# Two 1x1 convolutions of neighbouring blocks: seven products for eight in the earlier one too, and their matmuls taken in turn

## The chip, the cores and the metric

The kernel runs on one core of one Trainium2 chip. The metric is the device time of one execution in microseconds (us). All runs quoted here are with a mean granted TensorE clock of 0.98 unless another is given. Engine names in the profile: PE is TensorE's matmuls, PEld its weight loads, DVE is VectorE, ACT is ScalarE, POOL is GpSimd, SP is SyncE. L123 is a line of the kernel. A record is one matmul instruction of the trace; an fp32 matmul leaves two. PSUM is the memory that TensorE writes its sums to, in banks.

## The reference

Two bottleneck blocks on 64 images of 14x14 with 1024 channels, all in fp32, with batch statistics over images and pixels:

```python
def block(x, w1, b1, g1, be1, w2, b2, g2, be2, w3, b3, g3, be3, residual_scale):
    out = relu(_bn(_conv(x, w1, b1, 1, 0), g1, be1))     # 1x1, 1024 -> 256
    out = relu(_bn(_conv(out, w2, b2, 1, 1), g2, be2))   # 3x3, 256 -> 256
    out = _bn(_conv(out, w3, b3, 1, 0), g3, be3)         # 1x1, 256 -> 1024
    out = softplus(residual_scale)[0] * out
    return relu(x + out)
# ... the second block takes the first one's result
```

## The kernel before

The pixels are cut into 32 tiles of two images, 392 pixels each. A tile of `x` is 128 partitions x 8 channel groups x 392. The stages follow one another on TensorE: first convolution of block 0; 3x3 convolution; a transposing stage that forms the Gram matrix, from which the last convolution's statistics are computed before it is run; then the **fused stage**, in which the last convolution of block 0 is finished, added to `x`, and taken at once as input by the first convolution of block 1; then the 3x3 convolution, the transposing stage and the last convolution of block 1.

The last convolution in the fused stage is plain: eight output rows a tile, each from two matmuls, evicted by VectorE and ScalarE.

```python
def residual(psum, pool, b, t, w3, aff, made=()):
    scale, shift = aff
    xt = load_x(pool, b, t)
    yield xt
    for o in range(CS):                       # CS = 8
        ps = made[o] if o < len(made) else conv3(psum, t, o, w3)
        v = xt[:, o, :]
        nc.vector.scalar_tensor_tensor(v, ps, scale[:, o : o + 1], v, ALU.mult, ALU.add)
        nc.scalar.activation(v, v, AF.Relu, bias=shift[:, o : o + 1])
        # ... after the last row: write the tile
        yield xt
```

The first convolution already uses Winograd's form of Strassen's scheme: it treats a pair of tiles as the two columns of a 2x2 block product, and makes seven products, p1 to p7, instead of eight; each is four matmuls. Products p1, p6, p7 and p4 pile up on one PSUM bank, with a copy of the sum so far (a save) taken by ScalarE between them; p5 and p3 pile up on another.

```python
before, xn = None, next(rest)
for t in range(0, T, 2):                      # pairs of tiles
    # ... last convolution of tile t, p4 and p3 of the pair before
    now = Conv1(psum, pool, (xa, xb), (t, t + 1), w1, par[b + 1], stats1)
    # ... last convolution of tile t + 1
    now.p1(); now.p2(); now.p5(); now.t23(); now.p6()
    # ... first row of tile t + 2
    now.p7(); now.c22()
    before = now
```

## Time and profile before

| | before |
|---|---|
| time, median of 3 runs | 2219.84 us |
| first convolution, block 0, starts to 3x3 convolution's start | 7.1 to 320.8 us |
| 3x3 convolution to the start of the transposing stage | 320.8 to 667.1 us |
| transposing stage, statistics | 667.1 to 773.3 us |
| fused stage, first to last matmul | 773.3 to 1406.1, 632.8 us |
| what follows | 1406 to 2217 us |

The stage limits are the starts of the first matmuls of each stage in the trace. How the stage is bound, the prediction shows. In addition, three rows of the page's table of the costliest groups (line, engine, operation, out<-in, shapes, count, then busy time, mean ns of one, then idle time before them and what ended it). They hold both blocks' last convolutions: 512 output rows of 392 pixels in all, with 4 records each.

```profile
L126 PE MATMUL ps<-y,w 128*128 128x392 f32 x2048 | 685.6, 494 | 0.2 <-DVE x L515 0.2
...
L515 DVE SCALAR_TENSOR_TENSOR x<-ps,scale,x 128x392 f32<-128x392 f32 x512 | 316.0, 624 | 274.8 <-PE ps L126 273.5
L516 ACT ACTIVATE x<-x,shift 128x392 f32<-128x392 f32 x512 | 314.7, 622 | 435.5 <-DVE x L515 435.5
```

### The profile page before, as it was taken

Reading aid. Unit: us, or ns where it says so; the run is one execution under the profiler, and the core shown is the slowest. Engines: PE = TensorE matmul, PEld = TensorE weight load, DVE = VectorE, ACT = ScalarE, POOL = GpSimd, SP = SyncE. Lnnn points to the kernel's source line nnn. Section 1 sums busy time; section 2 is a strip of 40 time slices with the busy share of each in tenths; the row PEclk is TensorE's granted clock in tenths of the full one; section 3 lists DMA queues with packets and bytes.
Section 4 is the critical chain, followed back from the end, with each engine's and each line's share of the span. In section 5 each row is a group of like instructions: output and inputs, shape, how many; then the busy total and the mean of one; then the engine's idle time right before and its main releaser. Section 6 shows DMA issues by size and latency. Waiting matters only on the chain.

```text
span 2217.4 us, 22513 instructions
## 1 busy us (share of the span) xinstructions
PE 2144.0 (97%) x8984; PEld 1578.6 (71%) x8984; DVE 1343.1 (61%) x2091; ACT 585.8 (26%) x943; POOL 60.9 (3%) x126
## 2 busy tenths in 40 slices
PE   8999979999989999999999999799999799999997
PEld 5555559999988855555555555599999797555554
DVE  4766567787775455554555555678878534444443
ACT  1111142111105032332223323511111221444443
POOL 0100000000001000000000000000000000000000
PEclk9999989999999999999999999899999899999999
DMA  7755425555543443443434432355555401778884
GB/s 276 267 204 206 176 84 190 187 193 190 187 158 121 159 167 149 171 175 145 175 152 171 171 146 116 148 186 194 190 186 194 195 12 59 291 290 302 306 319 176
DMA packets 43977, 409.13 MB, mean 185 GB/s; under 512 B 5216, under 2 KB 5472, under 8 KB 11104
## 3 DMA queue, kind: packets, MB, share of 16 engines
q1 hardware_dynamic: 29376, 286.80, 35.9%
q0 software_dynamic: 13056, 118.50, 13.1%
q10 hardware_dynamic: 1440, 2.40, 0.3%
q8 instruction: 71, 1.16, 0.2%
q14 instruction: 34, 0.28, 0.0%
HBM read 289.18 MB, written 118.49 MB: 184 GB/s over the span
## 4 chain that ended last, share of the span: by engine, by line
PE 83%; issue 12%; DVE 2%; ACT 1%; POOL 1%; DMA 1%; POOLq 0%; ACTq 0%; DVEq 0%; SPq 0%
PE ps L126 19%; PE bu L126 15%; PE bp L126 7%; PE ps L343 6%; PE ps L349 6%; PE ps L338 6%; PE ps L345 6%; PE ps L351 6%; PE bx L126 4%; PE bx L439 4%; PE bp L440 2%; PE ps L451 2%; ACT y L264 1%; POOL out L519 1%; DVE spare L155 0%
## 5 line engine op out<-in xcount | busy, mean ns | idle before, releaser
L126 PE MATMUL ps<-y,w 128*128 128x392 f32 x2048 | 685.6, 494 | 0.2 <-DVE x L515 0.2
L126 PEld LDWEIGHTS ps<-y,w 128*128 128x128 f32 x2048 | 390.4, 191 | 285.9 <-issue 2.8
L515 DVE SCALAR_TENSOR_TENSOR x<-ps,scale,x 128x392 f32<-128x392 f32 x512 | 316.0, 624 | 274.8 <-PE ps L126 273.5
L516 ACT ACTIVATE x<-x,shift 128x392 f32<-128x392 f32 x512 | 314.7, 622 | 435.5 <-DVE x L515 435.5
L371 DVE TENSOR_TENSOR f<-ps,ms 128x448 f32<-128x448 f32 x192 | 113.2, 600 | 148.3 <-PE ps L351 81.8
L338 PE MATMUL ps<-sums,u 128*128 128x224 f32 (+1 forms) x768 | 172.1, 347 | 25.4 <-DVE sums L318 12.7
L126 PE MATMUL bu<-t,w1s 128*128 128x392 f32 x496 | 173.6, 493 | 1.3 <-ACT u L189 1.3
L343 PE MATMUL ps<-r,u 128*128 128x224 f32 (+1 forms) x768 | 173.6, 347 | 0.0
L349 PE MATMUL ps<-r,u 128*128 128x224 f32 (+1 forms) x768 | 172.8, 346 | 0.0
L338 PEld LDWEIGHTS ps<-sums,u 128*128 128x128 f32 x768 | 137.3, 190 | 26.8 <-issue 13.3
L345 PE MATMUL ps<-r,u 128*128 128x192 f32 (+1 forms) x768 | 154.1, 322 | 0.0
L351 PE MATMUL ps<-r,u 128*128 128x192 f32 (+1 forms) x768 | 153.3, 321 | 0.0
L362 ACT ACTIVATE ms<-ps 128x448 f32<-128x448 f32 (+1 forms) x80 | 41.9, 524 | 391.7 <-PE ps L338 391.7
L126 PEld LDWEIGHTS bu<-t,w1s 128*128 128x128 f32 x496 | 94.1, 190 | 71.0 <-ACT u L189 2.8
L343 PEld LDWEIGHTS ps<-r,u 128*128 128x128 f32 x768 | 141.8, 190 | 1.3
L349 PEld LDWEIGHTS ps<-r,u 128*128 128x128 f32 x768 | 136.7, 189 | 1.4
L345 PEld LDWEIGHTS ps<-r,u 128*128 128x128 f32 x768 | 132.9, 189 | 1.2
L351 PEld LDWEIGHTS ps<-r,u 128*128 128x128 f32 x768 | 131.8, 188 | 1.0
L189 ACT ACTIVATE u<-bu 128x392 f32<-128x392 f32 x93 | 46.2, 497 | 303.2 <-PE bu L126 303.2
L439 PE MATMUL bx<-zt 128*128 128x257 f32 x392 | 119.3, 386 | 4.1 <-DVE zt L453 4.0
L453 DVE TENSOR_TENSOR zt<-ps,crow 128x512 f32<-128x512 f32 x98 | 66.2, 690 | 93.3 <-PE ps L451 93.2
L264 ACT ACTIVATE y<-y,shift,scale 128x1568 f32<-128x1568 f32 x64 | 103.6, 1682 | 6.4 <-DVE shift L556 6.4
(134 smaller groups left out, 2115.3 us busy)
## 6 DMA issues: line engine op xcount, KB each, us to landing
u<-u SPq DMA_DIRECT2D x96, 1280.0 KB, 5.5
x<-in_x SPq DMA_DIRECT2D x62, 1568.0 KB, 6.7
mid<-x POOLq DMA_DIRECT2D x32, 1568.0 KB, 5.5
x<-mid SPq DMA_DIRECT2D x32, 1568.0 KB, 8.5
out<-x POOLq DMA_DIRECT2D x32, 1568.0 KB, 7.7
u<-y POOLq DMA_DIRECT2D x24, 320.0 KB, 5.9
u<-spare POOLq DMA_DIRECT2D x24, 320.0 KB, 3.0
x<-in_x SPq DMA_DIRECT2D x4, 784.0 KB, 7.2
```

The source lines that it names most:

```text
L126: tc.keep_in_program_order(nc.tensor.matmul(*args, **kw))
L264: nc.scalar.activation(y, y, AF.Relu, bias=shift[:, s : s + 1], scale=scale[:, s : s + 1])
L338: nc.tensor.matmul(m[:, o, :n], w(s, D1D2), sums[:, s].rearrange("p l c -> p (l c)"), start=(s == 0), stop=(s == MS - 1),)
L343: nc.tensor.matmul(odd, w(s, D1), r[:, s, :, WH:], start=(s == 0), stop=False)
L345: nc.tensor.matmul(odd[:, :, : WH - 1], w(s, D3), r[:, s, :, WH + 1 :], start=False, stop=(s == MS - 1))
L349: nc.tensor.matmul(even, w(s, D2), r[:, s, :, :WH], start=(s == 0), stop=False)
L351: nc.tensor.matmul(even[:, :, 1:], w(s, D0), r[:, s, :, : WH - 1], start=False, stop=(s == MS - 1))
L371: nc.vector.tensor_tensor(f[:, o].rearrange("p r (i q c) -> p q (r i) c", i=GI, q=2)[:, :, :lines], eos[o][:, :, :n].rearrange("p q (l c) ...
L439: nc.tensor.matmul(g0, zt[:, c, 0:P], zt[:, c, :], start=first, stop=last)
L453: nc.vector.tensor_tensor(zt[:, :, :M], tp.rearrange("p (c m) -> p c m", c=CH), crow[:, None, :].to_broadcast([P, CH, M]), ALU.subtract,)
L515: nc.vector.scalar_tensor_tensor(v, ps, scale[:, o : o + 1], v, ALU.mult, ALU.add)
L516: nc.scalar.activation(v, v, AF.Relu, bias=shift[:, o : o + 1])
```

## The change

The last convolution of the fused stage gets the seven-product scheme too, with the two halves of a tile (196 pixels) as columns and four groups of two output rows. The first convolution is done inside one tile as well. A product of the last convolution is a single matmul, so the products that pile up on one bank follow closely on each other. To give the saves time, the matmuls of the two convolutions are taken in turn, one of each, with the last convolution `LAG` = 12 steps ahead (after its first tile). In the changed kernel's profile, tiles whose names begin with `c` belong to the last convolution, those with `a` to the first; `cy` and `ay` are the banks of p1, p6, p7 and p4, `cx` and `ax` those of p2, `cp` and `ap` those of p5 and p3.

```diff
+LAG = 12
...
+    def stream(items):
+        before = None
+        for now in items:
+            yield from now.p1()
+            if before is not None:
+                yield from before.p3()
+                yield from before.p4()
+            yield from now.p6()
+            yield from now.p2()
+            yield from now.p5()
+            yield from now.p7()
+            before = now
...
+    class Conv3(Seven):
...
+        def after1(self):
+            self.saved(self.u12[:, : self.n], 0)        # ScalarE, 196
+        def after6(self):
+            self.saved(self.u12[:, self.n :], 0)        # ScalarE, 196
+        def after2(self):
+            self.add(0, 0, self.x)                      # VectorE, 196
+        def after5(self):
+            self.add(1, 1, self.p)
+        def after7(self):
+            u3 = self.saved(..., 1)
+            nc.gpsimd.tensor_add(self.part(1, 1), self.part(1, 1), u3)
+        def after3(self):
+            self.add(0, 1, self.p)
+            v = self.xt[:, self.o[0], :]
+            nc.gpsimd.tensor_add(v, v, self.u12)        # 392
+            self.relu(0)                                # ScalarE, 392
+        def after4(self):
+            self.add(1, 0, self.y)
+            self.relu(1)
...
+        a, c = stream(first_convs()), stream(last_convs())
+        step = 7 * CS // 2
+        for i in range(step + LAG):
+            next(c)
+        while True:
+            more = next(a, "end"), next(c, "end")
```

Besides: the first stage uses `stream` too, which changes the order of its products (before, p4 stood ahead of p3 there, and the next pair's p1 between p6 and p7); the fused stage's tiles are written by DMAs that ScalarE issues, before by GpSimd's; the row `crow` used in the transposing stage is no longer loaded with the parameters at the start but by its own DMA at that stage; the weights' sums for the seven products are made near the end of the transposing stage.

## The prediction

> **What bounds the kernel now.** I read the page's shares first, then the table of stretches of the fused stage (last convolution of block 0 with first convolution of block 1), then its timeline. TensorE is busy 97% of the span:
>
> ```profile
> PE 2144.0 (97%) x8984; PEld 1578.6 (71%) x8984; DVE 1343.1 (61%) x2091; ACT 585.8 (26%) x943; POOL 60.9 (3%) x126
> ```
>
> The stretches (TensorE, weight loads, VectorE, ScalarE, GpSimd busy us, clock, DMA) show the whole stage and one period of it, two tiles:
>
> ```profile
> 774.00:1407.00 633.00, 631.16 (x1912) 363.21 (x1910) 338.26 (x450) 189.31 (x321) 17.01 (x32) 1.00 0.40 155
> 845.21:884.71 39.50, 39.50 (x121) 22.80 (x121) 20.88 (x28) 11.85 (x20) 1.06 (x2) 1.00 0.44 163
> ```
>
> TensorE has no gap, at full clock; VectorE works 53% and ScalarE 30% of a period. A period is 32 matmuls of the last convolution and 28 of the first, 392 columns each; an fp32 matmul is two records, so 120 records in 39.50 us, 0.329 us a record. Sixteen periods are 632 us. Only fewer columns through TensorE can shorten this stage, and only while nothing stops TensorE.
>
> The timeline (start, duration, engine, line, instruction) gives the prices of what the change will use:
>
> ```profile
> 400.30 0.83 PE L351 MATMUL ps<-r,u 128*128 128x192 f32 x4
> 400.97 0.73 PE L338 MATMUL ps<-sums,u 128*128 128x168 f32 x4
> 401.54 0.74 PE L343 MATMUL ps<-r,u 128*128 128x168 f32 x4
> ...
> 779.69 3.29 DVE L515 SCALAR_TENSOR_TENSOR x<-ps,scale,x 128x392 f32<-128x392 f32 x6
> 780.34 3.29 ACT L516 ACTIVATE x<-x,shift 128x392 f32<-128x392 f32 x6 [1.72 <-DVE x L515]
> ...
> 1397.54 2.90 PE L126 MATMUL bu<-t,w1s 128*128 128x392 f32 x8 [0.65 <-ACT u L189]
> ```
>
> Starts of successive groups: 192 columns take 0.67/4 = 0.168 us a record, 168 take 0.57/4 = 0.143. So 196 columns are not limited by weight loads and take about 0.168. Six ReLUs back to back take 3.29 us and one 0.622 (page), so each further one 0.534. The last row is a product that accumulates on a bank and had to wait until ScalarE had saved the partial sum there: this dependence exists already, but with products of eight records it comes up only at the stage's end.
>
> The GpSimd hand-over, from VectorE's last write to GpSimd's start:
>
> ```profile
> 1755.43 0.86 DVE L402 TENSOR_TENSOR y<-fb,f 128x672 f32<-128x672 f32 x1
> ...
> 1756.48 0.19 POOL L433 MEMSET zt<- 128x2 f32 x4 [367.98 <-DVE y L402]
> ```
>
> 0.19 us. In the same timeline TensorE's handing over a bank to VectorE or ScalarE took 0.20 to 0.26 us after the next product's start, ScalarE to TensorE 0.05 (1397.49 to 1397.54) plus 0.10 for the exposed weight load (2.90 against 2.80 us), VectorE to ScalarE 0.03.
>
> **What the Trainium skill says.** "ScalarE: Activation LUTs", What ACT_TABLE_LOAD costs: 186 ns plus 0.833 ns an element, 93 ns more for each per-partition operand, and 93 ns of overlap back to back. For a ReLU of 392 that is 606 ns; the trace has 622, and an overlap of 88. For the new saves of 196 columns with a per-partition scale it gives about 0.44 us. "GPSIMD Engine Reference", 3.1: a two-input add takes about 2.6 cycles an element at 1.2 GHz. No GpSimd add is in this trace. My estimate from it: 392 elements 0.85 us plus the 0.10 that a tiny memset costs in the trace, 0.95 us; 196 elements 0.52. "TensorE: Matmul & The Clock Gate", table at the top: ScalarE, VectorE and GpSimd take their queues in strict order. The trace before neither contradicts nor tests it. "SBUF — State Buffer", Who interferes with whom: a VectorE instruction with two SBUF inputs contends with a GpSimd one that reads SBUF. Not shown here yet.
>
> **The change, part by part.**
>
> *Columns.* A tile's last convolution becomes 4 groups of 7 products, each one matmul of 196 columns: 28. The first convolution is now done inside one tile, 28 matmuls of 196. So 56 x 2 x 0.168 = 18.8 us a tile against 19.75; times 32, 602 against 632: 30 us less. That is 1.4%, and with nothing else it's all there is. The first stage keeps 28 matmuls of 392 a pair in another order; its gaps allow it, so zero. Combining the weights moves into the transposing stage, where VectorE was half idle; it frees some 2 us at the fused stage's start, but the first new save waits for the scale where eight plain matmuls ran on. Zero together.
>
> *Evictions.* For each group: 3 saves by ScalarE, 4 multiply-adds of 196 by VectorE (0.624 less 196/0.96 ns = 0.42 us each), 2 adds by GpSimd, 2 ReLUs. Per tile ScalarE gets 4 x (3 x 0.35 + 2 x 0.534) = 8.5 us plus 1.5 for the first convolution; VectorE 6 plus some 7; GpSimd 4 x 1.5 = 6. None is full in 18.8 us. Throughput isn't the trouble, order is.
>
> *The order.* The built program takes the two convolutions' matmuls strictly in turn, so a step of the last convolution is 0.67 us. Steps of a group n, with b the group before: p1(n), p3(b), p4(b), p6(n), p2(n), p5(n), p7(n). Products p1, p6, p7, p4 pile up on one bank, and each may start only after ScalarE saved the sum so far. ScalarE's queue of the built program reads, for nearly every group:
>
> ```
> save of p1(n); relu row 1 of b (waits GpSimd); relu row 2 of b; save of p6(n); save of p7(n)
> ```
>
> So the save that p7(n) needs stands behind two ReLUs, and the first of these waits for a GpSimd add that waits for VectorE. With 0 at the end of p3(b): VectorE starts at 0.23, done 0.65; GpSimd starts 0.84, done 1.79; first ReLU at 1.84; two ReLUs, 1.07: the save starts at 2.91, ends 3.35; TensorE goes on with p7(n) at 3.50. In a full pipeline p7(n) would start nine matmuls after 0, 9 x 0.336 = 3.02. A stall of 0.48 us in each group, and since the next p3 follows p7(n), it doesn't shrink: the period is 14 x 0.336 = 4.70 plus 0.48.
>
> To that: in two of four groups the queue holds a save or result of the first convolution before the p6 save too, 0.26 us, so 0.13 on average; at a tile's start VectorE's queue has the first convolution's 784-element sums (half of 1.79 us) between the adds, which I put at 0.3 us a tile, 0.08 a group; contention of those sums with GpSimd, 0.07 by guess. Sum 0.76 us a group.
>
> *Count.* 128 groups, of which about 6 run alone before the first convolution joins, and 122 in turn: 122 x 0.76 = 93 us. The six alone are nominally 7 x 0.336 = 2.35 us each, but the same chain (save of p7 behind the ReLUs, then p4) takes 3.5: 6 x 1.2, with the start 9 us. Net: -30 + 93 + 9 = +72, so 2220 + 72 = 2292 us.
>
> **The rivals.** (1) *The gain comes through.* The stall is a difference of two near numbers, 3.50 and 3.02. If the GpSimd add takes 0.5 us instead of 0.95, the save is ready in time, and the time is 2190 to 2205. For it: the add's duration is not in the profile, and whoever ordered the queues thought the ReLUs ready early. Against: in the groups of instructions GpSimd's one single-input operation on 128 elements a partition took 0.287 us, and a memset of 2 elements 0.10, which makes 1.5 ns an element and 0.69 us for 392 without the second input. That case leaves about 0.2 us, and 2255 us. (2) *VectorE's queue is the brake*: the add to a bank that p3 accumulates on stands behind sums that wait for the last ReLU of the tile. I count 0.3 us of it a tile; were it 1.5, 2330. (3) *GpSimd is the bound*: only if its adds average over 2.3 us (8 in 18.8); then the stage is over 700 us as well. (4) *DMA*: 0.44 of its share in a period; tile loads and writes stay, the writes issued by ScalarE. Not a bound.
>
> **Range and chances.** The GpSimd add decides: 0.1 us of it is 12 us of the kernel. 0.7 to 1.2 us gives 2260 to 2325. Below, I leave room for rival 1, above for rivals 2 and 3: 2215 to 2335. Faster by over 2% needs 44 us where 30 are on offer: 0.02. Within 2% (up to 2264): 0.31. Slower: 0.67.
>
> **What would show it.** Right: records of 196 columns 0.168 us apart where nothing waits; a wait of TensorE's `cy` bank on ScalarE's `cu` of near 0.5 to 0.8 us in nearly every group, some 90 us in all; ScalarE's ReLU waiting for GpSimd; TensorE near 85% busy in the stage; stage 700 us. Wrong: a GpSimd add of 0.5 us or less and TensorE still at 99%; or TensorE's waits put down to VectorE instead; or a changed time in another stage.

## The result, and the profile after

The changed kernel takes 2284.53 us (median of 4 runs, 2282.97 to 2284.69), against 2220.11 us (2219.68 to 2220.56) for the kernel before in the same rounds. Its ratio is 1.0289, with a 95% interval of 1.0271 to 1.0306: slower. A ratio here is the mean time of one kernel's fast runs over the mean of the other's in the same rounds, so it isn't quite the ratio of the medians.

The two traces, compared by the start of each stage's first matmul:

| | before | after | longer by |
|---|---|---|---|
| first convolution, block 0 | 313.7 | 318.2 | 4.5 |
| 3x3 convolution to transposing stage | 346.3 | 350.8 | 4.5 |
| transposing stage, statistics | 106.3 | 108.8 | 2.5 |
| fused stage, first to last matmul | 632.8 | 686.9 | 54.1 |
| the rest, to the end | 811.3 | 811.4 | 0.1 |

The first matmul came 0.4 us earlier, so the sum of 65.7 is 65.4 at the end (spans 2217.4 and 2282.8 us).

TensorE's shares, from the page of the changed kernel:

```profile
PE 2159.3 (95%) x10648; PEld 1804.8 (79%) x10648; DVE 1445.2 (63%) x2591; ACT 725.8 (32%) x1391; POOL 249.6 (11%) x350
```

The stretches of the fused stage (TensorE, weight loads, VectorE, ScalarE, GpSimd busy, clock, DMA), the whole and 50 us of it:

```profile
785.00:1471.00 686.00, 643.01 (x3581) 588.97 (x3580) 434.18 (x940) 328.37 (x768) 205.58 (x256) 0.99 0.37 144
1000.00:1050.00 50.00, 47.33 (x268) 43.58 (x267) 31.76 (x69) 24.58 (x59) 15.04 (x19) 1.00 0.42 162
```

Instead of 633 us without a gap there are 686 with 643 busy. Even this flatters TensorE. A product's busy time reaches 0.16 us beyond the next product's possible start (a pair of records takes 0.49 us and the next may start after 0.33), so a gap of that size isn't seen in it. Count records instead: 268 in 50 us, 0.187 us a record, where 0.166 us is the distance of undisturbed ones. That makes 11% of lost time, not the 5% that the busy share suggests.

What TensorE and the others waited for in the fused stage, from the table of waits (engine, tile, line, what released it: total us, times, longest):

```profile
ACT x L336 <- POOL x L357: 234.4, 127, 2.4
...
PEld cy L135 <- ACT cu L323: 59.3, 132, 3.5
...
PEld ap L135 <- issue: 21.3, 32, 1.3
PE cy L135 <- ACT cu L323: 17.9, 34, 2.9
...
PEld cp L135 <- DVE x L331: 14.3, 32, 0.5
PE ap L135 <- DVE y L273: 12.6, 32, 1.0
```

PEld and PE wait for the same thing at the same time, so their rows aren't to be added. I therefore took the matmul starts of the trace: each distance over 178 ns, less the 166 ns of an undisturbed record, put down to the tile of the later record.

| what TensorE was about to do in the fused stage | us lost | of it in the stage's beginning |
|---|---|---|
| last convolution's p6 and p7 (tile `cy`, combined weights): wait for ScalarE's saves | 53.4 | 7 |
| first convolution's p3 (tile `ap`): waits for VectorE's result of the same bank | 20.2 | |
| last convolution's p3 (tile `cp`): waits for VectorE's add of the same bank | 13.5 | |
| all else | 5.4 | |
| sum | 92.5 | |

The other 594.4 us are its 3584 records at 0.1658 us; together 686.9, which is the stage. Not all of the sum is waiting: up to 793 us the granted clock was 0.50, and 12 distances of 0.33 us there make about 2 us of it.

One group's chain, from the timeline (start, duration, engine, line, instruction). The prediction drew this chain from the built program and the prices of before:

```profile
1007.16 0.49 PE L135 MATMUL cp<-y,w3s 128*128 128x196 f32 x2
...
1007.70 0.42 DVE L331 SCALAR_TENSOR_TENSOR x<-cp,scale,x 128x196 f32<-128x196 f32 x1 [1.41 <-PE cp L135]
...
1008.20 1.01 POOL L357 TENSOR_TENSOR x<-x,cu 128x392 f32<-128x392 f32 x1 [0.73 <-DVE x L331]
...
1009.25 1.13 ACT L336 ACTIVATE x<-x,shift 128x392 f32<-128x392 f32 x2 [1.73 <-POOL x L357]
...
1010.29 0.40 ACT L323 ACTIVATE cu<-cy,scale 128x196 f32<-128x196 f32 x1
...
1010.74 0.30 PEld L135 LDWEIGHTS cy<-ct,w3s 128*128 128x128 f32 x2 [0.40 <-ACT cu L323]
1010.74 0.60 PE L135 MATMUL cy<-ct,w3s 128*128 128x196 f32 x2
```

Product p3 of the group before starts at 1007.16; VectorE adds it; GpSimd adds the saved row; ScalarE does two ReLUs; only then comes the save of the running sum (1010.29), and p7 starts at 1010.74. Ten matmuls after p3 it could have started at 1007.16 + 10 x 0.332 = 1010.48. The p6 product whose sum is saved here was at 1008.49, so the bank had been ready from about 1009.0. The save waited for the queue, not for its data.

Where the group stood in its tile made a difference: by the four groups of a tile, p7 lost 0.37, 0.37, 0.68 and 0.13 us on average between 830 and 1400 us. The 0.68 is the group with a result of the first convolution (0.31 us more in ScalarE's queue) in front of the save, as at 1003.92 to 1005.27 in the same timeline; the 0.13 is the group in which the first convolution's p3 had just been waited for.

The two groups of instructions that the chain is made of, from the page, with their means:

```profile
L336 ACT ACTIVATE x<-x,shift 128x392 f32<-128x392 f32 x256 | 148.1, 614 | 234.4 <-POOL x L357 234.4
...
L357 POOL TENSOR_TENSOR x<-x,cu 128x392 f32<-128x392 f32 x128 | 129.8, 1014 | 204.3 <-DVE x L331 204.2
```

Outside the fused stage, the 4.5 us ahead of the transposing stage go with one wait, again in the timeline:

```profile
663.38 0.46 ACTq L794 DMA_DIRECT2D crow<-in_par  x1
...
672.89 0.29 DVE L795 TENSOR_SCALAR crow<-crow 128x256 f32<-128x256 f32 x1 [4.83 <-DMA crow<-in_par]
```

Here VectorE's maximum on `crow` stands in its queue in front of the small instructions that make the scale for the whole stage, and `crow` takes 9 us from issue to use.

### The profile page after: what moved, and what is told of

It reads as the page before. It is cut to its first block, busy times and chain, and to the rows that moved or that the text cites. A ratio compares the mean times of both kernels' runs of the same rounds, so it can differ in the third digit from the quotient of the medians.

```text
span 2282.8 us, 27264 instructions
## 1 busy us (share of the span) xinstructions
PE 2159.3 (95%) x10648; PEld 1804.8 (79%) x10648; DVE 1445.2 (63%) x2591; ACT 725.8 (32%) x1391; POOL 249.6 (11%) x350
## 4 chain that ended last, share of the span: by engine, by line
PE 54%; issue 21%; DVE 9%; ACT 7%; POOL 6%; DMA 2%; ACTq 0%; POOLq 0%; DVEq 0%; SPq 0%
PE ay L135 8%; PE ps L465 6%; PE ps L460 6%; PE ps L471 6%; PE ap L135 5%; PE ps L467 5%; PE ps L473 5%; ACT x L336 5%; POOL x L357 4%; PE cy L135 4%; DVE x L331 3%; PE ax L135 2%; ACT cu L323 2%; PE bx L561 2%; PE cp L135 1%
## 5 line engine op out<-in xcount | busy, mean ns | idle before, releaser
L135 PE MATMUL ps<-y,w 128*128 128x392 f32 x1024 | 340.3, 495 | 0.0
L135 PEld LDWEIGHTS ps<-y,w 128*128 128x128 f32 x1024 | 195.8, 191 | 143.4 <-issue 2.7
L635 DVE SCALAR_TENSOR_TENSOR x<-ps,scale,x 128x392 f32<-128x392 f32 x256 | 160.3, 627 | 174.8 <-PE ps L135 154.7
L336 ACT ACTIVATE x<-x,shift 128x392 f32<-128x392 f32 x256 | 148.1, 614 | 234.4 <-POOL x L357 234.4
L135 PE MATMUL ay<-at,w1s 128*128 128x196 f32 (+1 forms) x752 | 209.3, 381 | 2.2 <-ACT au L259 2.2
L323 ACT ACTIVATE cu<-cy,scale 128x196 f32<-128x196 f32 x384 | 160.1, 418 | 109.0 <-PE cy L135 104.9
L331 DVE SCALAR_TENSOR_TENSOR x<-cp,scale,x 128x196 f32<-128x196 f32 x256 | 107.1, 418 | 109.2 <-PE cp L135 109.2
L135 PEld LDWEIGHTS ay<-at,w1s 128*128 128x128 f32 x752 | 136.3, 190 | 36.3 <-ACT au L259 3.2
L135 PE MATMUL cy<-ct,w3s 128*128 128x196 f32 x512 | 140.8, 357 | 23.2 <-ACT cu L323 17.1
L357 POOL TENSOR_TENSOR x<-x,cu 128x392 f32<-128x392 f32 x128 | 129.8, 1014 | 204.3 <-DVE x L331 204.2
L465 PEld LDWEIGHTS ps<-r,u 128*128 128x128 f32 x768 | 141.8, 190 | 1.3
L471 PEld LDWEIGHTS ps<-r,u 128*128 128x128 f32 x768 | 136.2, 188 | 1.4
L467 PEld LDWEIGHTS ps<-r,u 128*128 128x128 f32 x768 | 132.8, 189 | 1.2
```

What stands on the lines that cost most here:

```text
L135: tc.keep_in_program_order(nc.tensor.matmul(*args, **kw))
L323: nc.scalar.activation(v, self.y, AF.Identity, scale=self.scale[:, o : o + 1])
L331: nc.vector.scalar_tensor_tensor(v, bank, self.scale[:, o : o + 1], v, ALU.mult, ALU.add)
L336: nc.scalar.activation(v, v, AF.Relu, bias=self.shift[:, o : o + 1])
L357: nc.gpsimd.tensor_add(v, v, self.u12)
L465: nc.tensor.matmul(odd, w(s, D1), r[:, s, :, WH:], start=(s == 0), stop=False)
```

## The experiments

Twelve kernels, in three rounds. The changed kernel is the base unless another is named. All had 3 rounds beside the kernel before, whose medians there were 2221.40, 2220.67 and 2220.33 us. "Lost" is always by matmul starts, as in the table above.

### e1: ReLUs behind the save

```diff
         def after3(self):
             self.add(0, 1, self.p)
             nc.gpsimd.tensor_add(v, v, self.u12)
-            self.relu(0)
         def after4(self):
             self.add(1, 0, self.y)
-            self.relu(1)
-            self.end()
+        def late(self):            # called after p7 of the next group,
+            self.relu(0)           # and held in program order
+            self.relu(1)
+            self.end()
```

> The two ReLUs of a group are put behind the next group's p7 save in ScalarE's queue; nothing else is touched. Theory (order of ScalarE's queue): TensorE's wait for the save before p7, 46 us over the fused stage by the gaps between matmul starts, falls under 10 us, and the time by 35 to 50 us, to 2235 to 2250. Rival (VectorE's queue is the brake, the ScalarE waits only hide it): the waits move to the banks that VectorE reads and the time changes by less than 10 us. Rival (narrow matmuls are slow in themselves): no change.

Measured: 2245.37 us, ratio 1.0105 (1.0090 to 1.0120), and a **wrong result** (relative error 0.29), so this one is a look at the timing only. The fused stage took 648.3 us. From its table of waits:

```profile
PEld cp L135 <- DVE x L337: 41.4, 31, 1.4
...
PEld cy L135 <- ACT cu L329: 9.0, 14, 3.4
```

The loss at `cy` fell from 53.4 to 9.1 us and that at `ap` from 20.2 to 1.9; that at `cp` rose from 13.5 to 40.6. So the order in ScalarE's queue was the brake on p7; e7 repeats this with a correct result. The error comes from the first tile's first convolution having no p3 and p4 of a predecessor: its stream is eight matmuls shorter there, every later tile begins that much earlier, and by a count of the program's steps this is two steps before the last ReLUs of its tile are issued.

### e2: the row add on VectorE

```diff
-            nc.gpsimd.tensor_add(v, v, self.u12)
+            nc.vector.tensor_add(v, v, self.u12)
```

> The 392-element add of the saved sums goes from GpSimd to VectorE; ScalarE's queue keeps its order. Theory: the first ReLU becomes ready some 0.55 us earlier (about 0.55 us on VectorE for 0.08 hand-over and 1.01 on GpSimd), more than the stall of 0.35 to 0.4 us before p7, so that wait falls from 46 to under 10 us; VectorE gets 2.2 us more a tile, which may add up to 15 us to its own waits: 2235 to 2260. Rival (VectorE's queue is the brake): more work in it makes the kernel slower, 2290 to 2330.

Measured: 2256.73 us, ratio 1.0159 (1.0142 to 1.0176), correct; fused stage 659.5 us. The loss at `cy` fell to 10.3 us, at `ap` it doubled to 40.0, at `cp` it stayed at 12.2. Taking the GpSimd add out of the chain is worth about as much to p7 as moving the ReLUs, and the work comes back in VectorE's queue. The expectation's "keeps its order" isn't quite so: in the trace a result of the first convolution has changed places with a ReLU in ScalarE's queue once a tile, so this test is not of one link alone.

### e5: the first convolution's sums held in VectorE's order

```diff
-            nc.vector.tensor_sub(self.t3, self.b[1][1], self.b[0][1])
+            tc.keep_in_program_order(nc.vector.tensor_sub(self.t3, ...))
             # the same for t2 and t1
```

> The first convolution's sums t1 to t3 stand behind the previous item's result in VectorE's queue instead of before it. Theory: TensorE's wait for the bank ap before the first convolution's p3 goes, 18 to 20 us in the fused stage and 4 us in the first stage, the p7 waits stay near 46 us: 2258 to 2268. Rival: the wait only moves to the last convolution's banks, because the sums still wait for a ReLU with VectorE's queue behind them: within 8 us of 2284.

Measured: 2295.79 us, ratio 1.0335 (1.0319 to 1.0351), correct. Theory and rival both failed. The first stage lost 17 us more (the 3x3 convolution starts at 341.9 us instead of 324.9), and the fused stage gained only 3.8 (683.1): 17.0 us at `ap`, 23.5 at `cp`, 44.3 at `cy`. The trace doesn't bear out the rival's reason either: VectorE stands idle before none of the pinned sums (looked at from 6 to 342 and from 800 to 1400 us). In the first stage the results that the sums now stand behind wait for ScalarE's saves (69.0 us in 15 waits, in the changed kernel 4.6 in one), and TensorE waited for the late sums (13.3 us in 5 waits at `ay`). In the fused stage `ap` still waits with the sums behind it; e13 looks at that again. The edit also moved two pairs of ScalarE's instructions a tile, among them a save and a ReLU, so the smaller loss at `cy` is not the sums' alone.

### e6: the maximum of `crow` on GpSimd

```diff
-                    nc.vector.tensor_scalar(crow, crow, 0.0, None, ALU.max)
+                    nc.gpsimd.tensor_scalar(crow, crow, 0.0, None, ALU.max)
```

> The maximum of the separately loaded row is taken on GpSimd, so that VectorE's queue no longer waits for that load in front of the affine of the second normalization. Theory: the start of the first transposing stage moves back by 4.5 us, of the second by 0.6 us: 2278 to 2281. Rival: another load ends at the same time and nothing changes.

Measured: 2279.30 us, ratio 1.0259 (1.0244 to 1.0275), correct: 5.2 us less than the changed kernel, where the intervals of the ratios just overlap (1.0271 and 1.0275). From its timeline:

```profile
673.17 0.86 POOL L795 TENSOR_SCALAR crow<-crow 128x256 f32<-128x256 f32 x1 [11.34 <-DMA crow<-in_par]
```

The DMA is no quicker, but now an idle engine waits for it. The transposing stage starts at 671.0 instead of 675.7 us and the fused stage, at 687.2 us long as before, at 780.4 instead of 784.5. Of the 4.7 us 0.6 were given back: TensorE ran at a granted clock of 0.50 for the first 10 us of the stage (671 to 681), where in the changed kernel that took 5 us.

### e4: a lead of 19 instead of 12

```diff
-LAG = 12
+LAG = 19
```

> The changed kernel with one number altered: the last convolution runs 19 matmuls ahead of the first one's stream instead of 12, that is one group of seven more (the two streams keep their places against each other within a group). Theory: of the idle time of TensorE in the fused stage, only what comes from the tile boundary goes: the last convolution's p3 waiting for VectorE's add behind the sums (13.5 us) and some of the first convolution's p3 waiting for its result (20 us); the wait of p7 for ScalarE's saves behind the ReLUs (53 us with the start) stays between 42 and 56 us, so the fused stage takes 660 to 678 us and the kernel 2258 to 2276. Rival: the lead itself is what starves TensorE; then the p7 wait falls as well and the kernel takes under 2245. Second rival: the places within a period don't matter; 2280 to 2290. A fill that is 7 matmuls longer alone costs about 1 us in all of them. Results correct.

Measured: 2301.64 us, ratio 1.0366 (1.0349 to 1.0384), correct; fused stage 705.2 us. All three expectations failed. `ap` did fall to 2.8 us, but `cp` rose to 19.1 and `cy` from 53.4 to 82.5. By groups of a tile, p7 lost 0.37, 0.68 and 0.37 us as in the changed kernel, and in the group at the tile's boundary 1.09 instead of 0.13. That group in the timeline:

```profile
1020.53 0.49 PE L135 MATMUL cp<-y,w3s 128*128 128x196 f32 x2
1020.80 0.98 DVE L246 TENSOR_TENSOR at<-x 128x784 f32<-128x784 f32 x1 [1.67 <-PE ap L135]
...
1021.70 0.42 DVE L331 SCALAR_TENSOR_TENSOR x<-cp,scale,x 128x196 f32<-128x196 f32 x1
...
1022.25 1.01 POOL L357 TENSOR_TENSOR x<-x,cu 128x392 f32<-128x392 f32 x1 [4.67 <-DVE x L331]
```

VectorE waits 1.67 us to write the next tile's sum, because TensorE still reads the last tile's from the one buffer (tile `ap`); the add that p3 started (1020.53) stands behind that sum until 1021.70, and everything in the chain behind it is late by as much. The lead doesn't only decide how early a tile is ready; it decides what stands next to what in three queues.

### e7: e1 and e4 together

Late ReLUs and `LAG = 19`; no other edit. The ReLUs of a tile are then issued before the first convolution reads it.

> The late ReLUs of e1 and the lead of 19 together. In e1 the first convolution of a tile read the tile before its last ReLUs; with a lead of 19 they are issued before it, so the result must be correct now (relative error as that of the kernel before). Theory: the p7 wait stays under 12 us as in e1, the wait of the last convolution's p3 for VectorE (40.6 us in e1, because the sums in VectorE's queue waited for the late ReLUs) falls under 12, the wait of the first convolution's p3 under 8; the fused stage takes 608 to 626 us and the kernel 2205 to 2223. Rival: VectorE's queue still waits for the late ReLUs at each tile's start, since the sums are issued as soon as the tile's first convolution begins; then the p3 wait stays over 25 us and the kernel takes 2235 to 2255.

Measured: **2210.61 us**, ratio 0.9954 (0.9939 to 0.9969), correct. Fused stage 613.2 us, 19.6 less than before the change: 9.5 us lost at `cy`, 4.5 at `ap`, 1.5 at `cp`. The same stretch of 50 us as above, and then the group of the ReLUs:

```profile
1000.00:1050.00 50.00, 50.00 (x303) 49.66 (x302) 36.88 (x79) 26.39 (x64) 18.22 (x22) 1.00 0.44 166
```

```profile
L342 ACT ACTIVATE x<-x,shift 128x392 f32<-128x392 f32 x256 | 143.6, 610 | 0.7 <-POOL x L363 0.7
```

There are 303 records where the changed kernel had 268, and no gap. ScalarE's wait for GpSimd in front of the ReLUs went from 234.4 to 0.7 us. VectorE still waits for TensorE's reading of the sum as in e4 (40.1 us in 31 waits, 1.3 each), but no save stands behind what waits for it, and TensorE no longer feels it. Each half of this edit alone is a failure: 17 us slower, or a wrong result.

### e9: the row add on VectorE, with the lead of 19

The edits of e2 and e4 together.

> The lead of 19, and the row add of 392 on VectorE instead of GpSimd (as in e2). Theory: p7 wait 8 to 15 us as in e2; of e2's wait of the first convolution's p3 (40.0 us) and of the last one's (12.2) half goes with the lead: fused stage 625 to 645 us, kernel 2222 to 2242. Rival: the 40 us are due to the work that the adds put into VectorE's queue (4 x 0.5 us a tile) wherever the tile's boundary stands: 2248 to 2260. Results correct.

Measured: 2244.97 us, ratio 1.0109 (1.0093 to 1.0124), correct; fused stage 647.2 us, both just beyond the theory's upper ends, and under the rival's. `ap` fell from 40.0 (in e2) to 2.8 us, while `cy` rose from 10.3 to 28.2 and `cp` from 12.2 to 19.3. So the 40 us at `ap` hung on where the tile's boundary stood, but more than half of it came back elsewhere.

### e8: the ReLUs on GpSimd, with the lead of 19

```diff
-            nc.scalar.activation(v, v, AF.Relu, bias=self.shift[:, o : o + 1])
+            nc.gpsimd.tensor_scalar(v, v, self.shift[:, o : o + 1], 0.0, ALU.add, ALU.max)
```

> The lead of 19, and the ReLU moved from ScalarE to GpSimd (one tensor_scalar: plus shift, maximum with 0), which so does both row adds and ReLUs. Theory: ScalarE's queue then holds only saves and results that wait for TensorE alone, so the p7 wait falls under 12 us. GpSimd gets per group 1.01 + 0.60 + two ReLUs of 392 elements, which I put at 0.6 to 0.8 us each: 2.8 to 3.2 us of a group's 4.7, so it is not the bound. Fused stage 608 to 630 us, kernel 2205 to 2228. Rival: GpSimd's two ReLUs stand before the next group's add and before the bank of GpSimd's own order, and contention with VectorE slows its sums, so the waits for VectorE (first convolution's p3) grow over 30 us: 2240 to 2265. Results correct.

Measured: 2376.21 us, ratio 1.0700 (1.0684 to 1.0716), correct; fused stage 781.8 us, clock 0.958. Both expectations failed on one number:

```profile
L336 POOL TENSOR_SCALAR x<-x,shift 128x392 f32<-128x392 f32 x256 | 463.0, 1817 | 15.0
```

I had put this instruction at 0.6 to 0.8 us; it takes 1.82. A group then needs 1.01 + 0.60 + 2 x 1.82 = 5.25 us of GpSimd, against 14 matmuls x 0.332 = 4.65, so GpSimd alone makes the stage longer than before: 672 us for 128 groups. It was busy 43 of 50 us in the same stretch, and the stage took 781.8; what keeps it idle for the rest (it waits for VectorE and ScalarE before the add of 196) no run isolates. I had priced a two-step instruction like a one-step one.

### e10: the row add in two halves

The changed kernel with its lead of 12 and its ReLUs where they were; only the half row that is ready after p2 is added then, so that the add in p7's chain has 196 elements instead of 392.

```diff
         def after2(self):
             self.add(0, 0, self.x)
+            v = self.part(0, 0)
+            nc.gpsimd.tensor_add(v, v, self.u12[:, : self.n])
         def after3(self):
             self.add(0, 1, self.p)
-            v = self.xt[:, self.o[0], :]
-            nc.gpsimd.tensor_add(v, v, self.u12)
+            v = self.part(0, 1)
+            nc.gpsimd.tensor_add(v, v, self.u12[:, self.n :])
```

> The changed kernel, with GpSimd's add of a row of 392 cut in two: the first half row (196 elements) is added as soon as its product p2 is in, the second after p3 as before. So the add that the chain of p7 waits for takes 0.60 us (measured for the 196 of the same engine) instead of 1.014. Theory (the p7 wait is the rest of the chain add, two ReLUs, save): 0.41 us come off in each group, and the wait, 0.37 in most groups of the changed kernel, goes to nearly zero there and stays 0.2 to 0.3 in the one group of four where it was 0.68; the p7 wait falls from 53 to 5 to 20 us, the waits for VectorE stay (30 to 45 us), the fused stage takes 645 to 660 us and the kernel 2241 to 2258. Rival: GpSimd's order (now three adds a group, 1.8 us in all, the first of them in front of the one that matters) or its contention with VectorE eats the gain; 2265 to 2290. Results correct.

Measured: 2244.57 us, ratio 1.0110 (1.0095 to 1.0125), correct; fused stage 647.9 us. The `cy` loss fell from 53.4 to 15.0 us, `ap` and `cp` stayed (21.9 and 12.0). The add of the second half, from the groups of instructions:

```profile
L359 POOL TENSOR_TENSOR x<-x,cu 128x196 f32<-128x196 f32 x128 | 76.6, 598 | 107.3 <-DVE x L331 107.1
```

GpSimd does more in total (0.72 + 0.60 + 0.60 us a group, was 1.01 + 0.60), and the kernel is 40 us shorter: 0.416 us less in the chain of each group. This is the test that I trust most, as it leaves the orders of TensorE and ScalarE alone (in the trace one pair of ScalarE's instructions at the start has changed places) and changes the length of one link.

### e13: the first convolution's sums behind its results

```diff
                 yield from before.p3()
+            now.prepare()          # the three sums of Conv1, until now in __init__
+            if before is not None:
                 yield from before.p4()
# ... and the sums and the results of Conv1 held in program order
```

> The changed kernel, with the first convolution's three sums of 784 elements asked for after its p3 and held in VectorE's order behind its results (in the changed kernel two of them stand before the result of bank ap). Theory: the first convolution's p3 waits because VectorE's result of bank ap stands behind sums that in turn wait for the last ReLU; with the sums behind it that wait (20.2 us) falls under 4 us. The sums now have only the four matmuls of p4 (2.7 us) to be ready for p6, about 2.4 us of work with an add between, so a wait of ay on them of up to 0.5 us a tile may appear (0 to 15 us). Fused stage 660 to 685 us, kernel 2258 to 2283. Rival: the wait is not VectorE's order but ap's own products being late; then ap stays near 20 and the kernel is at 2284 or above. Results correct.

Measured: 2325.22 us, ratio 1.0470 (1.0453 to 1.0488), correct, clock 0.975. The first stage, whose sums are of 1568 elements and now come too late, lost 55 us (3x3 convolution from 379.9 instead of 324.9 us): a cost I had not thought of, though e5 had shown it at 17 us. The fused stage can still be read: 674.4 us. Of the theory, the loss at `cp` went (13.5 to 0.7 us), but the one it was made for did not: `ap` 17.0 instead of 20.2, with 17.5 new at `ay`, where p6 waits for the late sums. Its timeline shows why `ap` stays:

```profile
1108.72 0.50 PE L135 MATMUL cp<-y,w3s 128*128 128x196 f32 x2
...
1109.26 0.42 DVE L338 SCALAR_TENSOR_TENSOR x<-cp,scale,x 128x196 f32<-128x196 f32 x1 [1.93 <-PE cp L135]
1109.60 0.41 DVE L280 SCALAR_TENSOR_TENSOR y<-ap,par,au 128x196 f32<-128x196 f32 x1
...
1110.15 0.57 PE L135 MATMUL ap<-x,w1s 128*128 128x196 f32 x2 [0.27 <-DVE y L280]
```

VectorE was idle for 1.93 us, and the result of `ap` (L280), whose product and ScalarE's save were there since about 1107.7, stood behind the last convolution's add (L338), which waited for its p3. My theory that the sums were in the way is refuted as the main cause; the place behind p3's add is enough. The trace of e5 has the same picture (VectorE idle for 1.94 us, the add at 1010.84, the result of `ap` at 1011.18, the sums only after it).

### e11: e7, with e6, and with p4 ahead of p3 in the first stage

```diff
-    def stream(items):
+    def stream(items, four_first=False):
...
+                if four_first:
+                    yield from before.p4()
+                    yield from before.p3()
...
-        for _ in stream(items()):
+        for _ in stream(items(), True):
```

> Towards a version that beats both: e7 (late ReLUs, lead 19; 2210.6) with the crow maximum on GpSimd (e6, 4.8 us there) and, in the first stage alone, p4 before p3 as in the kernel before. Theory: the stages are separate, so the gains add up: transposing stage starts 4.8 us earlier relative to the second convolution, and the first stage gets back 2 to 4 us of its 4.1, since VectorE's result of bank ap has four more matmuls' time. Fused stage unchanged at 613. Kernel 2201 to 2206. Rival: the first stage's 4 us come from elsewhere (the filter pieces on VectorE) and stay: 2205 to 2208. Results correct.

Measured: **2202.80 us** (2201.72 to 2204.01), ratio 0.9923 (0.9908 to 0.9937), correct. The fused stage is as in e7 (613.0 us); the transposing stage starts 11.3 us after the last matmul of the 3x3 convolution instead of 16.3; the 3x3 convolution starts at 322.8 us, so the first stage got back 2.1 us of the 4.1 by which that start had slipped. This version beats both kernels, the one before by 0.8%.

### e12: e11, with the weights' sums on GpSimd

```diff
-                        beside[NT - 5] = lambda: weights.extend((combine_w1(one, w1), combine_w3(one, w3)))
+                        beside[NT // 2] = lambda: weights.extend((combine_w1(one, w1, nc.gpsimd), ...))
```

> e11 with the eight weight combinations (512 elements each) on GpSimd in the middle of the transposing stage instead of on VectorE near its end. Theory: the transposing stage got 2.6 us longer through them; GpSimd has nothing to do there and needs about 8 x 1.25 = 10 us; 1.5 to 2.6 us come back: kernel 2198 to 2204, 1.5 to 2.6 under e11. Rival: contention of GpSimd with VectorE in the transposing stage lengthens it by as much; within 1 us of e11. Results correct.

Measured: 2203.01 us, ratio 0.9922 (0.9907 to 0.9936), correct; the same as e11. From the first transposing matmul to the fused stage 109.8 us in both, but not because the sums on VectorE cost nothing. The first matmul of the statistics comes 98.3 us after the stage's start in e11 and 96.8 in e12, so 1.5 us were gained there. They were lost again at the stage's end: its last 48 records, small matmuls of the statistics, and the wait for VectorE behind them took 6.27 us in e11 (771.72 to 777.99) and 7.72 in e12 (770.72 to 778.44). The granted clock was 1.00 up to 776 us in e11, and 0.50 from 774 us on in e12, whose profiled execution was the slowest of its four (2203.85; the fastest took 2200.60). So the rival's number came true, but not by its reason. With what the stage has in e11 over the 106.3 us of before goes a lower clock too, 0.50 and 0.56 in its first two stretches of 5 us (0.66 and 1.00 before).

## Why the prediction was right or wrong

The predicted time of 2292 us is 7.5 over the 2284.53 measured, and slower was the right side. By its steps:

- **Columns.** Predicted 0.168 us a record, 602 us in all, 30 less than before. Undisturbed records are 0.166 us apart: 594.4, so 38 less. Right in kind, and off by 8 us: 0.168 came from a single difference of 0.67 us over four records, which is rounded to 0.01.
- **Prices.** A multiply-add of 196 took 0.418 us (0.42 predicted), a save 0.418 (about 0.44), a GpSimd add of 392 1.014 (0.95). Two slips had no effect: 16 multiply-adds of 0.42 are 6.7 us a tile and not 6, and GpSimd adds of 2.35 us would make a stage of 602 us, not of over 700.
- **The order: p7 waits for its save behind two ReLUs that wait for GpSimd.** This mechanism is shown three ways: by moving the ReLUs (e1, e7), by taking GpSimd out (e2, with the blemish named there), and by shortening one link (e10). The links were predicted well. With 0 at 1007.47 in the chain above, predicted and measured: VectorE done 0.65 and 0.65; GpSimd starts 0.84 and 0.73, ends 1.79 and 1.74; save starts 2.91 and 2.82, ends 3.35 and 3.22; p7 3.50, and 3.27 plus the 0.10 by which its first record is longer. So a wait of 0.37 and not of 0.48 us. Two terms were mis-sized: GpSimd's start after VectorE (0.08 us, I had 0.19 from a hand-over after another kind of work) and the 0.13 us for the first convolution's instructions in ScalarE's queue. The latter cost 0.31 in one group of four, and the tile's other waits gave 0.24 back in another, so it was 0.02 on average: 0.386 us a group measured against 0.61.
- **The sum of the waits.** Predicted: 122 x 0.61 = 74 for p7, and 9 for the start, together 83; measured at `cy` 53.4, the start included. Sums ahead of VectorE's adds at a tile's start: predicted about 10, measured 13.5. Contention with GpSimd: predicted 8.5 by guess. The longer sums are there (1.32 against 0.97 us), but no loss of TensorE is to be put down to them alone. The first convolution's p3 on `ap`: not foreseen, measured 20.2. All else 5.4. So 102 predicted and 92.5 measured, with one term much too big and one missing.
- **VectorE's queue as a rival.** I gave it 0.3 us a tile; at `ap` and `cp` it is (20.2 + 13.5) / 32 = 1.05. The step that failed looked at p3 of the last convolution and not at p3 of the first, which piles up on a bank in the same way.
- **Other stages: zero.** This step was wrong by 11 us. The `crow` load was in the diff, and I priced neither its 9 us nor its place in front of the affine; e6 shows 4 to 5 us of it. In the first stage the order of p3 and p4 was worth 2.1 us (e11); the other 2 us are open. Of the 2.5 us in the transposing stage the weights' sums are about 1.5 (e12), where the prediction let them cost nothing; with the rest goes a lower granted clock (0.50 against 0.66 in the stage's first 5 us, 0.84 against 0.98 in its last stretch), which no run isolates.
- **The total.** The fused stage was predicted 72 us longer and is 54; the others zero, and are 11. The 18 and the 11 partly cancel, which is why the total is closer than its parts.
- **"0.1 us of the GpSimd add is 12 us."** e10 took 0.416 us off and gained 40 us, 9.6 for each 0.1. It is less than 12 because the wait can't fall below zero and had only 0.37 in most groups.
- **TensorE near 85% busy.** The table of stretches has 643 of 686 us, 94%. The lost time is 92.5 of 686.9, 13%: the claim was about right for lost time, and the busy share is the wrong view for it.
- **The gain of the columns.** Predicted as what is left if nothing stops TensorE. e7 has 613.2 us, 19.6 less than before of the 38 on offer; 19 are still lost, about half of it at `cy` in the first groups, which run alone.

## What to carry to other kernels

When an operation is split into pieces that pile up on one bank, put the save that the next piece needs ahead of everything in its queue that waits for other engines; draw the chain link by link before choosing an order, and count the matmuls that the order leaves to cover it. A change of lead or of order moves the neighbours in every queue at once: e4 alone lost 17 us and e1 alone read unfinished rows, and together they gained 74. Judge TensorE's losses by the distances between the starts of its records, as the busy share hides gaps as short as a product's tail.

## What the Trainium skill lacked or had wrong

- "GPSIMD Engine Reference", 3.1: its rate for an add holds. The runs show 1.014 us for 392 elements and 0.603 for 196, so 2.1 ns an element (the page's 2.6 cycles at 1.2 GHz are 2.17) and 0.19 us fixed, where I had estimated 0.10. It gives no rate for a tensor_scalar of two steps with a per-partition operand: e8 shows 1.817 us for 392 elements, 1.8 times the add.
- "SBUF — State Buffer", Who interferes with whom: it calls the contention of VectorE with GpSimd an exclusive lock, and the runs nearly agree. A VectorE sum of 784 elements with two SBUF inputs takes 0.97 us alone. In e7 one that started while a GpSimd add had 0.52 us to go (1003.22; the add ran from 1002.72 to 1003.74) took 1.35 us; in e5 those that started with 0.90 us to go (L244) took 1.74. So a sum lost all but some 0.13 us of the time that the add still ran, a remainder that the section doesn't mention. The other way round it is alike: GpSimd's add of 196 at 1012.37 in e5 started with 0.88 us of such a sum to go and took 1.33 us instead of 0.60.
